# Taking the gathers of adjT's columns out of the first pass over the adjacency matrix

## The chip, the cores and the metric

The kernel runs on one core of one Trainium2 chip. The metric is the device time in microseconds (us), the median over several executions; lower is better. The engines are named as in the profile: PE is TensorE (PEld its weight loads), DVE is VectorE, ACT is ScalarE, POOL is GpSimd, SP is SyncE. "PEclk" or "clock" is the TensorE clock that was granted, as a share of full speed.

## The reference

The network has two layers over a graph of 3327 nodes with 512 features. `adj` is a dense 3327 x 3327 float32 matrix whose entries are almost all zero. What matters of it:

```python
h = jnp.maximum(_layernorm(x), 0.0)                    # layer 0: a plain GCN, dense adj used twice
h0 = jax.nn.relu(adj @ (h @ W1) + b1)                  # first pass over adj
x = x + adj @ (h0 @ W2) + b2                           # second pass over adj

h = jnp.maximum(_layernorm(x), 0.0)                    # layer 1: attention over the non-zeros of adj
hs = h @ W_sa
scores = (hs @ a_l)[:, None] + (hs @ a_r)[None, :]
e = jnp.where(adj != 0, jnp.exp(-leaky_relu(scores, 0.01)), 0.0)
attn = e / (e.sum(1, keepdims=True) + 1e-5)
x_a = attn @ hs
x_b = adj @ (h @ W_gcnb) + b_gcnb
...                                                    # two gates from adj @ h and h; cut
x = x + jax.nn.sigmoid(attn_a * x_a + attn_b * x_b)
```

## The kernel before

It works in three stages.

*Pass 1* streams the transposed matrix in column chunks of 512 (7 chunks of 26 tiles) and multiplies it. From the tiles DVE also takes, per row and group of 64 columns, the largest absolute value. Out of that, while the next chunk streams, the kernel makes *lists*: for each of 52 groups of 64 columns, which rows have any non-zero there. The lists of chunk c cover 8 groups; each group has 3 to 16 slots of 128 rows, 231 slots in all.

*Pass 2* streams the matrix again and makes `h` for layer 1, which is stored to HBM row by row (`h_dram`).

*Layer 1* is sparse. For each slot GpSimd gathers 128 rows of `h` (2080 bytes each) by an indirect DMA, and PE multiplies them with the values of adjT in that group. Those values, 64 columns of 128 listed rows (256 bytes each), have been gathered ahead of time into `adj_c`: one indirect DMA per slot, 231 as well. They are called *column gathers* below, and those of `h` *row gathers*.

In the kernel before, a column gather is written down as soon as its list is:

```python
def make_lists(c, most):
    ...                                               # flags, counts, offsets; cut
    for batch in batches:                             # groups of this chunk
        ...
        nc.vector.tensor_copy(row_h[:, f0 : f0 + m], jb[:, :m])
        nc.vector.scalar_tensor_tensor(               # row_a: rows of adjT seen as (j, group) rows
            row_a[:, f0 : f0 + m], jb[:, :m], float(NG), group_col[:, f0 : f0 + m],
            op0=ALU.mult, op1=ALU.add,
        )
        for b in batch:
            for k in range(room[b]):
                r = first[b] + k
                gather(adj_c[b][:, k, :], adj_groups, row_a[:, r : r + 1], NP * NG - 1)
        yield
```

Both passes take a step of the lists after a tile. Pass 2 also makes a block of `h` of the chunk before after every fifth tile, with four scores on DVE:

```python
for c in range(NCH):                                  # pass 1
    for j in range(NB):
        a = load_adj(j, c, "a1")
        nc.tensor.matmul(acc[:, :w], u[j], a[:, :w], ...)
        nc.vector.tensor_reduce(most[:, : w // GW, j], ..., op=ALU.max, apply_absolute_value=True)
        ...
        if j >= 2:
            next(lists, None)                         # lists of chunk c - 1
    ...

for c in range(NCH):                                  # pass 2
    for j in range(NB):
        a = load_adj(j, c, "a2")
        nc.tensor.matmul(acc[:, :w], g[j], a[:, :w], ...)
        if c == 0 and j >= 2:
            next(lists, None)                         # lists of the last chunk
        ...

def make_h1(c, sT):                                   # per block of 128 rows, in pass 2
    ...
    nc.sync.dma_start(h_dram[i * P : (i + 1) * P, :], h)
    for s, k in ((0, 0), (2, 1), (3, 2)):
        score(i, h[:, :D], s, node[i][:, k : k + 1])  # DVE, two 128x512 operands
```

In layer 1 the gathered rows go through a ring of 10 buffers, and the blocks of 128 nodes are taken in an order of their own:

```python
for c in range(n):
    hr = h_rows[taken % NH]                           # NH = 10
    taken += 1
    r = first[b] + c0 + c
    gather(hr, h_dram[:, :], row_h[:, r : r + 1], NP - 1)
    ...

blocks = [*range(1, NB // 2), 0, *range(NB // 2, NB)]
```

## Time and profile before

| | before |
|---|---|
| time, median of 3 runs | 941.31 us (936.98 to 942.03) |
| the profiled run, its span | 1143.1 us, 1141.4 us |
| busy in that span | PE 76%, DVE 56%, POOL 46%, ACT 17% |
| mean granted clock in it | 0.882 |
| column gathers (231) in that trace | start at 103.5, end at 473.3 us |
| `h` stored completely | 649 us, when the first row gather starts |
| indirect DMA, start to start | 1.30 us |

The span in 40 equal slices of 28.5 us, busy share of each in tenths:

```profile
PE   5788406356364754999999369899999789999995
...
POOL 6842766575564645400000166556555555544410
...
DMA  7688216345362543999998665556445543545421
```

Pass 1 fills slices 1 to 15. Its PE digits fall to 0 and 3 although PE is what it works with, and the DMA is low in the same slices, while POOL, which from the fifth slice on does nothing there but gather columns, keeps its 4 to 7. Slices 16 to 22 are pass 2; from the 17th, in which the last column gathers end, PE stands at 9 and the DMA at 8 or 9. The zeros of POOL there are its wait for `h`. The rest is layer 1. The profiled run is 202 us longer than the median of the timed ones.

### The profile page before, as it was taken

What the parts mean: (1) busy time and instruction counts of PE and PEld (TensorE: products, weight loads), DVE (VectorE), ACT (ScalarE), POOL (GpSimd) and SP (SyncE); (2) the same over time, 40 slices, a digit from 0 to 9 for tenths busy, and PEclk for the clock granted to TensorE, in tenths of its full rate; (3) what the DMA queues carried; (4) which work ended last, traced back from release to release, by engine and by line L of the source; (5) the groups of instructions that cost most, each with busy time, mean ns of one, the idle gap of its engine ahead of it and who ended that gap; (6) DMA issues with size and microseconds to landing.
All of it is one profiled execution on the core that took longest, in us unless ns stands there. A gap on an engine that the chain in (4) does not pass through costs nothing.

```text
span 1141.4 us, 10611 instructions
## 1 busy us (share of the span) xinstructions
PE 870.3 (76%) x2750; PEld 427.7 (37%) x2750; DVE 640.3 (56%) x1732; ACT 195.6 (17%) x449; POOL 528.3 (46%) x583
## 2 busy tenths in 40 slices
PE   5788406356364754999999369899999789999995
PEld 4564102122121331434344224445544345455552
DVE  6467205236161652366665645777777466777775
ACT  4460000000000000111111112222222122222221
POOL 6842766575564645400000166556555555544410
PEclk9999757577595876999999679999999889999998
DMA  7688216345362543999998665556445543545421
GB/s 240 219 281 287 73 38 213 85 137 163 89 200 80 171 138 103 301 339 362 340 358 297 197 182 145 152 152 182 138 133 156 141 138 100 147 128 149 131 69 40
DMA packets 107445, 199.62 MB, mean 175 GB/s; under 512 B 19516, under 2 KB 26894, under 8 KB 107376
## 3 DMA queue, kind: packets, MB, share of 16 engines
q1 hardware_dynamic: 74880, 129.64, 34.5%
q0 software_dynamic: 25872, 58.20, 18.6%
q10 hardware_dynamic: 6624, 11.02, 2.8%
q8 instruction: 24, 0.39, 0.1%
q14 instruction: 45, 0.37, 0.1%
HBM read 182.32 MB, written 27.37 MB: 184 GB/s over the span
## 4 chain that ended last, share of the span: by engine, by line
PE 52%; another core or an unknown queue 17%; DMA 11%; DVE 10%; issue 5%; POOL 3%; ACT 1%; SPq 0%; POOLq 0%; DVEq 0%; ACTq 0%
PE acc L555 13%; PE acc_g L456 11%; PE p_a L586 8%; PE p_b L586 7%; PE acc_u L371 6%; DMA a<-in_adjT_dram 5%; DVE most L372 4%; PE px L429 2%; POOL h_rows L249 2%; DMA h_rows<-h_rows,row_h 2%; PE p_s L578 2%; PE ptt L566 2%; DMA xb<-x 1%; DMA x<-in_x_dram 1%
## 5 line engine op out<-in xcount | busy, mean ns | idle before, releaser
L249 POOL DMA_INDIRECT h_rows<-h_rows,row_h x231 | 239.7, 1038 | 375.5 <-DMA h_rows<-hrow 176.1
L249 POOL DMA_INDIRECT adj_c<-in_adjT_dram,row_a x231 | 230.9, 999 | 159.5 <-issue 76.1
L555 PE MATMUL acc<-h_rows,ae 128*128 128x512 f32 x462 | 216.6, 612 | 26.5 <-DVE ae L520 19.4
L371 PE MATMUL acc_u<-a,u 128*128 128x512 f32 (+1 forms) x364 | 193.0, 663 | 5.3 <-ACT u L184 3.4
L456 PE MATMUL acc_g<-a,g 128*128 128x512 f32 (+1 forms) x364 | 158.4, 582 | 8.0 <-DMA a<-in_adjT_dram 6.0
L555 PEld LDWEIGHTS acc<-h_rows,ae 128*128 128x128 f32 x462 | 87.8, 196 | 129.8 <-issue 117.5
L372 DVE TENSOR_REDUCE most<-a 128x8 f32<-128x512 f32 (+1 forms) x182 | 112.7, 639 | 18.4 <-DMA a<-in_adjT_dram 14.8
L514 DVE TENSOR_SCALAR ae<-s_left,h_rows 128x64 f32<-128x64 f32 x231 | 55.9, 262 | 87.4 <-DMA h_rows<-h_rows,row_h 78.8
L456 PEld LDWEIGHTS acc_g<-a,g 128*128 128x128 f32 x364 | 66.7, 193 | 90.1 <-issue 48.6
L586 PE MATMUL p_a<-W_sa_sb,tyT 128*128 128x512 f32 x208 | 99.6, 622 | 0.0
L586 PE MATMUL p_b<-W_g_sb,tyT 128*128 128x512 f32 x208 | 93.5, 592 | 0.0
L321 PE MATMUL p_list<-step,at 128*128 128x27 bf16 x231 | 17.4, 184 | 94.6 <-DVE at L316 44.9
L371 PEld LDWEIGHTS acc_u<-a,u 128*128 128x128 f32 x364 | 70.2, 219 | 51.1 <-issue 40.8
L508 DVE RECIPROCAL va<-vb 128x512 f32<-128x512 f32 x26 | 87.2, 3353 | 0.9
L417 DVE SCALAR_TENSOR_TENSOR junk<-hrow,w_rows 128x512 f32<-128x512 f32 x104 | 71.8, 690 | 3.5 <-DMA x<-x 0.3
L321 PEld LDWEIGHTS <-at 128*128 128x128 bf16 x231 | 15.2, 105 | 140.9 <-issue 59.8
L193 PE MATMUL pg<-ident,gT 128*128 128x128 f32 x26 | 6.2, 376 | 75.1 <-ACT gT L190 54.8
L190 ACT ACTIVATE gT<-acc_u,b_col 128x512 f32<-128x512 f32 (+1 forms) x7 | 4.6, 657 | 332.4 <-remote 241.6
L586 PEld LDWEIGHTS p_b<-W_g_sb,tyT 128*128 128x128 f32 x208 | 39.5, 190 | 49.9 <-issue 49.9
L431 DVE TENSOR_TENSOR x<-px,xb 128x512 f32<-128x512 f32 x26 | 17.8, 683 | 70.4 <-PE px L429 70.4
L519 ACT ACTIVATE ae<-ae 128x256 f32<-128x256 f32 (+1 forms) x70 | 26.2, 379 | 170.9 <-DVE ae L518 93.4
L586 PEld LDWEIGHTS p_a<-W_sa_sb,tyT 128*128 128x128 f32 x208 | 38.8, 197 | 38.5 <-issue 38.5
(108 smaller groups left out, 894.3 us busy)
## 6 DMA issues: line engine op xcount, KB each, us to landing
a<-in_adjT_dram SPq DMA_DIRECT2D x312, 256.0 KB
h_rows<-hrow SPq DMA_DIRECT2D x26, 260.0 KB
x<-in_x_dram SPq DMA_DIRECT2D x26, 256.0 KB
xb<-x SPq DMA_DIRECT2D x26, 256.0 KB
xb<-xb SPq DMA_DIRECT2D x26, 256.0 KB
a<-in_adjT_dram SPq DMA_DIRECT2D x52, 128.0 KB
x<-x ACTq DMA_DIRECT2D x26, 256.0 KB
x1b<-x SPq DMA_DIRECT2D x26, 256.0 KB
```

The costliest lines, as they stand in the source:

```text
L249: nc.gpsimd.indirect_dma_start(out=dst, out_offset=None, in_=table, in_offset=bass.IndirectOffsetOnAxis(ap=rows, axis=0), bounds_check=las ...
L321: nc.tensor.matmul(plv[:, first[b] - f0 + s0 + k, :], at[:, k * P : (k + 1) * P], step[:, b - g0, :], start=True, stop=True,)
L371: nc.tensor.matmul(acc[:, :w], u[j], a[:, :w], start=(j == 0), stop=(j == NB - 1))
L372: nc.vector.tensor_reduce(most[:, : w // GW, j], a[:, :w].rearrange("p (b i) -> p b i", i=GW), axis=AX.X, op=ALU.max, apply_absolute_value ...
L417: nc.vector.scalar_tensor_tensor(junk, h, 1.0, w_rows[:, s, :], op0=ALU.mult, op1=ALU.mult, accum_out=into)
L429: nc.tensor.matmul(px, sT[:, b * P : (b + 1) * P], W2_sb, start=True, stop=True)
L456: nc.tensor.matmul(acc[:, :w], g[j], a[:, :w], start=(j == 0), stop=(j == NB - 1))
L508: nc.vector.reciprocal(va, vb)
L514: nc.vector.tensor_scalar(e, s_l, s_r, LEAST_SCORE, op0=ALU.add, op1=ALU.max)
L519: nc.scalar.activation(e, e, AF.Exp, scale=-1.0)
L555: nc.tensor.matmul(acc, ae[:, c, :], hr[:, :D], start=(c0 + c == 0), stop=(c0 + c == room[b] - 1),)
L586: nc.tensor.matmul(p, tyT[:, k, s, :], w_sb[:, k, :], start=(k == 0), stop=(k == KD - 1))
```

## The change

The intent: the column gathers share the DMA engines with pass 1's loads, in whose stretch the profile shows the holes. So none of them is to lie in pass 1. The column gathers become a generator, in the order in which layer 1 will want them. Of the 231, the first, of the last group (whose list is made at the start of pass 2), is a marker; 140 are drawn behind it, and the other 90 one after every second row gather of layer 1.

```diff
+EARLY = 140
...
+    def gather_adj():
+        for b in groups[-1:] + groups[:-1]:
+            for k in range(room[b]):
+                r = first[b] + k
+                yield gather(adj_c[b][:, k, :], adj_groups, row_a[:, r : r + 1], NP * NG - 1)
+
+    columns = gather_adj()
...                                                   # in make_lists:
-                for b in batch:
-                    for k in range(room[b]):
-                        r = first[b] + k
-                        gather(adj_c[b][:, k, :], adj_groups, row_a[:, r : r + 1], NP * NG - 1)
...                                                   # in pass 2, c == 0, after the last lists:
+                with tc.issue_after(next(columns).ins):
+                    for _ in range(EARLY):
+                        next(columns)
...                                                   # in combine:
                     gather(hr, h_dram[:, :], row_h[:, r : r + 1], NP - 1)
+                    if taken % 2 == 0:
+                        next(columns, None)
```

`issue_after` binds only the 140 to the marker. Nothing binds the other 90, and the scheduler is free to move those forward as far as their inputs allow.

More of the change, by code (lines that the diff above doesn't have):

```diff
@@ L116, in ln_relu, with gather @@
         nc.scalar.activation(dst, src, AF.Relu, bias=ln[:, 4:5], scale=ln[:, 3:4])
+    def gather(dst, table, rows, last):
+        return nc.gpsimd.indirect_dma_start(
+            out=dst, out_offset=None, in_=table,
+            in_offset=bass.IndirectOffsetOnAxis(ap=rows, axis=0),
+            bounds_check=last, oob_is_err=False,
+        )
+    adj_groups = adjT.rearrange("j (b i) -> (j b) i", i=GW)
+    blocks = [*range(1, NB // 2), 0, *range(NB // 2, NB)]
+    groups = [2 * i + k for i in blocks for k in range(2)]
+    def gather_adj():
[4 more added lines that the diff above has]
+    columns = gather_adj()
     with (
@@ L246, in make_constants @@
                 nc.gpsimd.memset(t, 0.0)
-        def gather(dst, table, rows, last):
-            nc.gpsimd.indirect_dma_start(
-                out=dst, out_offset=None, in_=table,
-                in_offset=bass.IndirectOffsetOnAxis(ap=rows, axis=0),
-                bounds_check=last, oob_is_err=False,
-            )
-        adj_groups = adjT.rearrange("j (b i) -> (j b) i", i=GW)
         def make_lists(c, most):
@@ L596 @@
         turning, weighing = None, None
-        blocks = [*range(1, NB // 2), 0, *range(NB // 2, NB)]
-        for n, b in enumerate(2 * i + k for i in blocks for k in range(2)):
+        for n, b in enumerate(groups):
             if b % 2 == 0:
```

## The prediction

> **What bounds the kernel now.** I read the times before the page. The three plain runs have a median of 941.3 us; the profiled run took 1143.1 us with a span of 1141.4 us. Profiling itself therefore added about 202 us, and the first thing to find out is where. The chain that ended last, by engine:
>
> ```profile
> span 1141.4 us, 10611 instructions
> ...
> PE 52%; another core or an unknown queue 17%; DMA 11%; DVE 10%; issue 5%; POOL 3%; ACT 1%; SPq 0%; POOLq 0%; DVEq 0%; ACTq 0%
> ```
>
> On one core there is no other core. The same chain in order of time puts every long piece of that 17% (194 us) between 117 and 452 us; the longest (start, length):
>
> ```profile
> 136.28 34.94 another core or an unknown queue
> ...
> 280.87 27.51 another core or an unknown queue
> ...
> 335.50 27.14 another core or an unknown queue
> ...
> 392.23 18.01 another core or an unknown queue
> ```
>
> Stretches of the core, one stalled, one clean, both in pass 1, and one in pass 2 (columns as the first line names them):
>
> ```profile
> core 0: us, PE busy (x) PEld busy (x) DVE busy (x) ACT busy (x) POOL busy (x), PEclk, DMA share, GB/s
> 135.00:172.00 37.00, 4.90 (x8) 1.91 (x8) 2.08 (x6) 0.69 (x1) 23.92 (x24) 0.55 0.16 40
> ...
> 310.00:335.00 25.00, 23.73 (x81) 9.92 (x79) 21.87 (x51) 0.00 (x0) 12.53 (x13) 0.93 0.75 230
> ...
> 505.00:535.00 30.00, 28.92 (x69) 12.03 (x68) 19.27 (x59) 5.36 (x11) 0.00 (x0) 1.00 1.00 358
> ```
>
> In the stall nothing but the gathers moves. PE's last matmul is recorded as ending at 140.0, yet its semaphore steps on at 140.4, 145.3, 150.9 and 171.2, and all others wait for those steps. These stalls look like gathers hurting pass 1, and are surely what the change is aimed at. But 1141 - 194 = 947, and a plain run, less the 1.7 us by which the profiled time exceeds its span, is 939.6. So I choose to read the stalls as made by profiling, not as time of the plain kernel.
>
> The plain timeline, then, worked out from the trace. Layer 1 runs from its first gather of rows at 649.4 to 1141.4, 492 us, so in a plain run h is complete at 939.6 - 492 = 448. Pass 1 ends at 426.1 in the trace; of the 194 us, 176 lie before that, so plain at about 249. Without stalls PE (23.7 of 25 us) and DVE (21.9) bound pass 1, with the DMA at 0.75. Pass 2 is bound by DMA (share 1.00 at 358 GB/s). Layer 1 begins bound by GpSimd's gathers and soon by PE.
>
> The gathers:
>
> ```profile
> L249 POOL DMA_INDIRECT h_rows<-h_rows,row_h x231 | 239.7, 1038 | 375.5 <-DMA h_rows<-hrow 176.1
> L249 POOL DMA_INDIRECT adj_c<-in_adjT_dram,row_a x231 | 230.9, 999 | 159.5 <-issue 76.1
> ...
> 111.51 1.00 POOL L249 DMA_INDIRECT adj_c<-in_adjT_dram,row_a  x1 [0.30 <-issue]
> 112.82 0.99 POOL L249 DMA_INDIRECT adj_c<-in_adjT_dram,row_a  x1 [0.32 <-issue]
> ...
> 649.38 1.00 POOL L249 DMA_INDIRECT h_rows<-h_rows,row_h  x1 [176.12 <-DMA h_rows<-hrow]
> ```
>
> Successive starts lie 1.30 us apart, so 231 cost GpSimd 231 x 1.303 = 301 us. In the trace they end at 473.3, and GpSimd then waits 176 us for h. That slack is partly the profile's: in a plain run the gathers go from 103.5 without a break (the lists of later column chunks come faster than GpSimd works them off) to about 405, leaving 448 - 405 = 43 us. Also, only (249 - 103.5) / 1.303 = 112 of the 231 lie under pass 1 even before the change.
>
> **What the Trainium skill says.** "Perfetto Trace Analysis", section "GPSIMD Engine Instruction", calls GpSimd's spans unreliable and advises start-to-start spacing; I use 1.303 us instead of the row's 999 ns. Its section "Tensor Engine Instruction (MATMUL, LD_WEIGHTS)" says that a matmul's end is estimated; the trace agrees, with semaphore steps up to 31 us after the recorded end. "DMA: Bandwidth & Descriptors", section "Issuing engines are not separate DMA queues", says that DMAs of all issuers share the same 16 engines; so a gather in a full pass 2 takes time from the loads. In the stall 23 gathers took 8.1% of 16 engines' time over 35 us, 0.123 us of all engines each.
>
> **The change part by part.** Of PE, DVE, ScalarE and SyncE the built program keeps every instruction in its place; GpSimd has the same instructions, and only the 231 gathers of adj are reordered. What matters is where the scheduler put them, and it is not what the change says: all 231 still stand before the first gather of rows. Only the 140 bound to the marker gather of the last group are held back. The 90 free ones had inputs early and were hoisted to the front. The new order: 7 of group 1, then 74 of groups 26 to 47, then the marker's group and the others held back (141 in all), then 9. So 81 stay in pass 1's part of the queue, none goes between layer 1's gathers.
>
> 1. GpSimd loses time. The 7 can start at 108.9 (group 1's list) and end at 118. The next need the list of chunk 3, made while chunk 4 streams. From the last matmul of chunk 0 (91) to 249 there are 5.5 chunks, 28.7 us each; chunk 3 is loaded at 91 + 3 x 28.7 = 177, and the list of group 26 takes some 7 of 26 steps more: 185. GpSimd idles from 118 to 185, 67 us, while in the kernel before it was gathering groups 0 to 25.
> 2. From 185 the other 224 follow without a break: 74 take 96 us, more than the lists of chunks 3 to 5 need; the marker's list is then done. The end is 185 + 224 x 1.303 = 477.
> 3. The first gather of rows stands behind them in the same queue, so it starts at 477 instead of 448: +29 us on the path.
> 4. Given back: before, the first gather of rows took 7.2 us until DVE used it (649.4 to 656.6), beside the weights' loads and the last scores, against 3.4 us for a later one (666.4 to 669.8). With those out of the way some 4 us return.
> 5. DMA: before, 231 - 112 = 119 gathers lay beyond pass 1; after, 231 - 7 - (249 - 185) / 1.303 = 175 do. The 56 more cost pass 2 56 x 0.123 = 7 us, which delays h to 455. This lies beside GpSimd's later end, so it is not added. Pass 1 isn't DMA-bound and gains at most a few us.
>
> Layer 1 can't make up a late start: its early blocks wait for gathers at 1.30 us each, and then PE runs gapless, so a shift passes to the end. Sum: 941.3 + 29 - 4 = 966. I take 3 us off for a gather's spacing that may be a little shorter in a plain run: **963 us**.
>
> **The rivals.**
> - The stalls are real in plain runs, and taking gathers out of pass 1 removes them. For: they occur only while gathers run. Against: 947 fits 939.6 without them; for a plain run to hold them, the rest would have to run 200 us faster, though pass 2 is already at 358 GB/s and PE at full granted clock. Were 40 us of them left, the two gather-free chunks might save 15 us: about 925 without the late start of layer 1.
> - The gathers are hidden anyway. If the plain spacing were 1.17 us, the end would be 185 + 262 = 447, and only the 7 us of DMA in pass 2 would show: 945 to 948. For: the profile slows other things, so perhaps GpSimd. Against: spacing is 1.30 both inside stalls and in clean stretches, for both kinds of gather.
> - Gathers slow down beside a full DMA. Each waits for the landing of the eighth before it. Against: the last ones, at 465 to 473 in pass 2, kept 1.30. Were they 1.4, the end would be 499 and the time about 985.
>
> **Range and chances.** The time is 941 plus the larger of two delays: DMA (about 5) and GpSimd's end (224 x spacing + 185 - 448, less 4). A spacing of 1.2 to 1.33 gives 943 to 970; uncertainty in the 448 and 185 adds some 8 either way. Range 940 to 977. The border of 2% is 960.1, near my estimate: slower 0.56, same 0.39, faster 0.05.
>
> **What would show it.** In the profile after: about 81 gathers ahead of pass 2 or at its edge, with a long idle stretch of GpSimd after the first 7; no gather of adj between gathers of rows; the wait of the first gather of rows for h (176 us before) gone or short, since the queue is late instead; chunks 1 and 2 of pass 1 free of the unknown waits, which reappear where the gathers now are. The profiled span may even shrink while the plain time grows. I am wrong if the plain time falls below 930 (stalls were real), or if GpSimd still waits long for h in a plain-length timeline (gathers cheaper than 1.30 us).

## The result, and the profile after

The changed kernel takes **975.08 us** (973.69 to 975.74, 4 runs) against 940.65 us (936.98 to 942.03, 4 runs). A ratio in this document is the mean time of one kernel's fast runs over that of the other's of the same rounds, so it is not quite the ratio of the medians: here 1.037, with a 95% interval of 1.0338 to 1.0403. The change makes the kernel slower. Its profiled run took 975.2 us, no longer than the timed ones.

The span, and the chain that ended last, by engine and by line, from the page of the changed kernel:

```profile
span 973.5 us, 10580 instructions
...
PE 49%; issue 16%; POOL 15%; DMA 12%; DVE 6%; ACT 1%; SPq 0%; POOLq 0%; DVEq 0%; ACTq 0%
PE acc L570 15%; POOL adj_c L120 11%; PE acc_u L381 10%; PE p_a L601 8%; PE p_b L601 8%; DMA a<-in_adjT_dram 5%; DMA h_rows<-h_rows,row_h 4%; PE p_s L593 2%; POOL h_rows L120 2%; PE ptt L581 2%; DMA x<-in_x_dram 1%; DMA xb<-x 1%; DVE most L382 1%; DVE va L521 1%; POOL x L187 1%
```

The 17% of "another core or an unknown queue" is gone. In its place stand POOL's column gathers (11%) and "issue" (16%), which alternate: followed piece by piece, the chain goes from one column gather to the next all the way from 249 to 485 us. The 40 slices, now of 24.3 us:

```profile
PE   4778999998999999880047899999978999999994
...
POOL 6951200377777777777767545646455564454400
...
DMA  7688898997999999984156544555464444544410
```

PE and DMA have no holes in pass 1 (slices 1 to 10), and pass 2 (slices 10 to 18) is full too. Then PE has two slices, the 19th and 20th, with hardly any work (digits 0 and 0), while POOL goes on at 7. That is the new piece. The stretches, with columns as in the prediction's table of stretches:

```profile
91.00:120.00 29.00, 26.86 (x127) 11.95 (x126) 27.29 (x74) 0.69 (x1) 7.25 (x7) 1.00 0.89 288
265.10:297.80 32.70, 31.11 (x73) 12.63 (x72) 19.95 (x61) 5.67 (x11) 25.39 (x25) 1.00 1.00 347
320.00:400.00 80.00, 73.88 (x173) 30.10 (x172) 49.86 (x157) 15.19 (x30) 62.03 (x60) 1.00 1.03 353
446.00:485.00 39.00, 0.00 (x0) 0.00 (x0) 0.00 (x0) 1.48 (x2) 29.86 (x31) 0.50 0.27 70
790.00:890.00 100.00, 100.00 (x328) 51.22 (x326) 77.57 (x182) 26.25 (x62) 47.48 (x46) 1.00 0.47 136
```

The first is chunk 1 of pass 1, with 7 column gathers, the second chunk 1 of pass 2, the third the middle of pass 2: DMA share 1.03 and 353 GB/s with 60 gathers in 80 us, so pass 2 was full as before. From 446 to 485 PE and DVE do nothing at all and GpSimd gathers 31 times. `h` was complete by then (the last store was issued at 443.2). Later PE is busy for all of 100 us, so a late start of layer 1 isn't made up there. GpSimd in the order of time, where its first long idle ends:

```profile
117.17 0.99 POOL L120 DMA_INDIRECT adj_c<-in_adjT_dram,row_a  x1 [0.30 <-issue]
183.07 1.00 POOL L120 DMA_INDIRECT adj_c<-in_adjT_dram,row_a  x1 [64.91 <-DVE at L330]
184.38 1.00 POOL L120 DMA_INDIRECT adj_c<-in_adjT_dram,row_a  x1 [0.31 <-issue]
```

After the seventh gather GpSimd waits 65 us for the list of the next group in its queue. And where the columns end and the rows begin:

```profile
483.68 1.00 POOL L120 DMA_INDIRECT adj_c<-in_adjT_dram,row_a  x1 [0.30 <-issue]
484.98 1.00 POOL L120 DMA_INDIRECT h_rows<-h_rows,row_h  x1 [0.30 <-issue]
486.29 1.00 POOL L120 DMA_INDIRECT h_rows<-h_rows,row_h  x1 [0.30 <-issue]
```

The first row gather waits 0.30 us, as any gather does behind another. In the profile of before it waited 176 us for `h`. The groups of gathers, as the page has them (busy time, mean ns of one, idle before and what ended most of it):

```profile
L120 POOL DMA_INDIRECT h_rows<-h_rows,row_h x231 | 238.8, 1034 | 197.5 <-PE acc L570 114.7
L120 POOL DMA_INDIRECT adj_c<-in_adjT_dram,row_a x231 | 240.9, 1043 | 160.9 <-issue 68.0
```

The column gathers' mean is 1043 ns, against 999 ns in the profile of before.

### The profile page after: what moved, and what is told of

It is laid out like the page before. It is cut to its first block, busy times and chain, and to the rows that moved or that the text cites. A ratio compares the mean times of both kernels' runs of the same rounds, so it can differ in the third digit from the quotient of the medians.

```text
span 973.5 us, 10580 instructions
## 1 busy us (share of the span) xinstructions
PE 831.2 (85%) x2750; PEld 412.6 (42%) x2750; DVE 637.1 (65%) x1732; ACT 195.7 (20%) x449; POOL 537.4 (55%) x583
## 4 chain that ended last, share of the span: by engine, by line
PE 49%; issue 16%; POOL 15%; DMA 12%; DVE 6%; ACT 1%; SPq 0%; POOLq 0%; DVEq 0%; ACTq 0%
PE acc L570 15%; POOL adj_c L120 11%; PE acc_u L381 10%; PE p_a L601 8%; PE p_b L601 8%; DMA a<-in_adjT_dram 5%; DMA h_rows<-h_rows,row_h 4%; PE p_s L593 2%; POOL h_rows L120 2%; PE ptt L581 2%; DMA x<-in_x_dram 1%; DMA xb<-x 1%; DVE most L382 1%; DVE va L521 1%; POOL x L187 1%
## 5 line engine op out<-in xcount | busy, mean ns | idle before, releaser
L120 POOL DMA_INDIRECT h_rows<-h_rows,row_h x231 | 238.8, 1034 | 197.5 <-PE acc L570 114.7
L120 POOL DMA_INDIRECT adj_c<-in_adjT_dram,row_a x231 | 240.9, 1043 | 160.9 <-issue 68.0
L381 PE MATMUL acc_u<-a,u 128*128 128x512 f32 (+1 forms) x364 | 164.3, 581 | 8.0 <-ACT u L207 4.8
L466 PE MATMUL acc_g<-a,g 128*128 128x512 f32 (+1 forms) x364 | 156.7, 573 | 10.3 <-DMA a<-in_adjT_dram 9.4
L601 PE MATMUL p_a<-W_sa_sb,tyT 128*128 128x512 f32 x208 | 96.8, 607 | 0.0
L381 PEld LDWEIGHTS acc_u<-a,u 128*128 128x128 f32 x364 | 60.8, 190 | 49.2 <-issue 31.7
L187 POOL TENSOR_TENSOR x<-x,b_row 128x512 f32<-128x512 f32 x26 | 33.0, 1280 | 24.5 <-ACT h L117 13.0
L575 ACT COPY ty<-acc 128x512 f32<-128x512 f32 x52 | 30.2, 582 | 61.7 <-PE acc L570 61.5
L204 PE MATMUL pu<-W_sb,hT 128*128 128x128 f32 x208 | 30.7, 294 | 9.3 <-ACT hT L198 9.2
L581 PEld LDWEIGHTS ptt<-ident,ty 128*128 128x128 f32 x208 | 26.3, 142 | 27.8 <-issue 25.1
```

Of the source, the lines that this page charges most:

```text
L120: return nc.gpsimd.indirect_dma_start(out=dst, out_offset=None, in_=table, in_offset=bass.IndirectOffsetOnAxis(ap=rows, axis=0), bounds_ch ...
L187: nc.gpsimd.tensor_tensor(xs[i], xs[i], b2_row, ALU.add)
L204: nc.tensor.matmul(pu[:, :HID], hT[:, k, :], W1_sb[:, k, :], start=(k == 0), stop=(k == KD - 1))
L381: nc.tensor.matmul(acc[:, :w], u[j], a[:, :w], start=(j == 0), stop=(j == NB - 1))
L466: nc.tensor.matmul(acc[:, :w], g[j], a[:, :w], start=(j == 0), stop=(j == NB - 1))
L581: nc.tensor.transpose(pt[:, k * P : (k + 1) * P], ty[:, k * P : (k + 1) * P], ident)
```

## The experiments

My theory after the result: the kernel lost its time because the late queue of gathers delays the first row gather, as predicted, and the size was off because gathers ran at 1.35 us instead of 1.30. Rivals: the cost is in the moved code or order rather than in the late queue; the gathers slow down because the DMA is full; and the holes in the profile of before are real and would be worth something.

The runs went to four chips: 15, 4, 2 and 5. **The kernel before took 1131 to 1142 us in all timed runs on chip 15, 928 to 941 on chip 4, 1141 to 1148 on chip 2 and 1130 to 1144 on chip 5.** All of those are labelled "fast", since that label compares a run with the fastest of the same kernel in the same call. I call a chip *stalling* where the kernel before takes some 1140 us, and *free of stalls* where it takes some 935; kernels are compared only within a call. The record of the prediction (937 to 942) is of the second kind.

### On stalling chips: first call (chip 15)

**Before again**, unchanged, one look:

> The kernel before, unchanged, profiled once more. If the 194 us of waits on an unknown queue were an accident of the first profiled execution or of profiling, this profile may show a span near 939 us: then I expect the last column gather to end at about 405 to 412 us, h to be complete (first gather of rows) at 447 us (give or take 4), and a wait of 35 to 43 us of GpSimd before it. If the stalls belong to this order of gathers whenever it is profiled, the span is again above 1100 us with most waits in pass 1. If they were real in plain runs, the plain time could not be 941.

1128.53 us for the run whose profile was kept. The seven timed runs of the same kernel beside it took 1131.12 to 1142.47 us. So the kept profile is no longer than the runs that are timed on the same chip, and my reading of the first profile's holes is not borne out: by their length the timed runs of this chip have them too. (Each of these runs lists a span and a granted clock. So the record does not say of any of them that nothing was recorded while it ran, and whether recording has a part in the stalls stays open.) Pass 1 ends at 415.3 us in this trace and `h` is complete at 637.7, much as in the profile of before (426.1 and 649.4). That profile therefore looks like one of a stalling chip, while the times beside it are of a chip free of stalls.

**No hold**, the changed kernel with the 231 gathers drawn at once, so that each goes as soon as its list is there:

```diff
-                with tc.issue_after(next(columns).ins):
-                    for _ in range(EARLY):
-                        next(columns)
+                for _ in columns:
+                    pass
```

> The changed kernel, with nothing held behind the marker gather: all 231 column gathers are free at the same place of the code, and the scheduler puts them in the order in which lists are ready, without an idle stretch, nearly as in the kernel before. If the late start of layer 1 (GpSimd idle for 66 us, then 224 gathers in a row) is the whole loss, this is 940 us (936 to 945, ratio 0.995 to 1.005). If another part of the change costs the time (code moved, gathers beside pass 2), it stays near 975.

1125.29 us, ratio to before 0.9901 (0.9844 to 0.9958). The gathers run from 103.7 to 461.9 without a long idle (13.2 us at most), pass 1 ends at 416.7, `h` is complete at 636.1: as before. It is 1% faster than the kernel before on this chip, by more than its interval; on chip 2 (below) it is not.

**Hold 125** and **hold 110** hold back fewer, and draw the rest right after them:

```diff
-EARLY = 140
+EARLY = 125      # and 110
...
                     for _ in range(EARLY):
                         next(columns)
+                for _ in columns:
+                    pass
```

> 125 held instead of 140: 15 more column gathers (of groups 0 and 1) run at once when their list is ready, in GpSimd's idle stretch. 209 instead of 224 are left at 183 us, so at 1.348 us each the queue ends at 465 instead of 485 and the time is 955 (952 to 959): 20 us less than the changed kernel, 1.35 us per gather. If the loss comes from DMA traffic in pass 2, 15 gathers fewer there give 1 to 2 us: 973.

> 110 held: 29 instead of 7 gathers run before 183 us, 202 are left, the queue ends at about 455 and the time is 945 (941 to 949); it can't get below 940 since h is complete only at about 446. If the loss comes from DMA traffic in pass 2, about 972.

1153.91 us, 1.0142 (1.0068 to 1.0216), and 1148.55 us, 1.0113 (1.005 to 1.0176). Their absolute numbers miss by some 200 us, because the expectations were written for a chip free of stalls. Nor can the dose be read from the ratios: on this chip the gathers end at 501.2 and 495.7 us, but `h` is complete only at 662.3 and 654.5, so the queue's lateness costs nothing, and what differs is when `h` is complete, 17 to 25 us later than in the kernel before (637.7). The series was made to measure the late queue, and didn't.

### On a chip free of stalls: second call (chip 4)

The kernel before took 935.6 us there (928.21 to 940.9, 7 runs).

**Small groups first.** The kernel before with layer 1's blocks in another order. Those with few slots (and so less GpSimd time per unit of PE work) go first:

```diff
-        blocks = [*range(1, NB // 2), 0, *range(NB // 2, NB)]
+        blocks = [*range(NB // 2, NB), *range(1, 7), 0, *range(7, NB // 2)]
```

> The kernel before with layer 1's blocks in another order: those of 3 and 4 columns first, then blocks 1 to 6, 0, 7 to 12. It tests the claim that layer 1 starts bound by GpSimd's gathers at 1.3 us each and that PE is gapless afterwards: with few gathers per block PE gets its matmuls by the weights at once. If so some 20 us of the start are saved: 920 us (910 to 932). If the start's idle PE is latency that any order has, 938 to 945.

934.61 us (931.41 to 939.01), ratio 0.9989 (0.9926 to 1.0053): no gain, a miss. PE was indeed busier at the start of layer 1, 57.96 us of the first 71.6 against 47.47 of the first 72 in the changed kernel. It lost that again later, and layer 1 took 488.9 us against 488.5. So my step "then PE runs gapless" was too simple: layer 1's length did not react to a better beginning.

The run is worth more as a view of the kernel before free of stalls, since nothing ahead of layer 1 differs from it. GpSimd at the end of the columns:

```profile
412.94 0.99 POOL L249 DMA_INDIRECT adj_c<-in_adjT_dram,row_a  x1 [0.30 <-issue]
448.39 0.99 POOL L249 DMA_INDIRECT h_rows<-h_rows,row_h  x1 [34.45 <-DMA h_rows<-hrow]
```

The columns end at 413.9 us, GpSimd waits 34.45 us for `h`, and the first row gather starts at 448.4. That is the timeline that the prediction worked out from the stalled trace (end at about 405, 43 us of slack, `h` at 448). Set beside the changed kernel's 485.0, it gives the shift: 36.6 us, against a measured 34.4 us (975.08 - 940.65). The other stages leave no room for a second loss: pass 1 ends at 241.7 us here and at 239.6 in the changed kernel, the last store of `h` is issued at 445.5 and 443.2, and layer 1 takes 488.9 and 488.5. What differs is the time between the last store and the first row gather, 2.9 us here and 41.8 there. That answers the rival of the moved code, although "no hold" was never run on a chip free of stalls.

**No column gathers** at all in the kernel before (wrong; the relative error is 0.046):

```diff
-                for b in batch:
-                    for k in range(room[b]):
-                        r = first[b] + k
-                        gather(adj_c[b][:, k, :], adj_groups, row_a[:, r : r + 1], NP * NG - 1)
```

> Wrong result on purpose: the kernel before without any column gather (the compact columns stay zero). It bounds what any placement of the gathers can win. If they lie wholly beside other work and cost only DMA share under pass 2 (chunks of pass 2 took 30 us beside gathers in the changed kernel's profile, 28.4 without in the profile of before), 934 us (929 to 940). If gathers in pass 1 really stall it, as the profile of before suggests, well below 920.

930.56 us (924.47 to 935.64), ratio 0.9942 (0.9865 to 1.002). All 231 together cost the kernel before about 0.6% (the interval includes nothing at all), and by the interval's lower end no more than 1.4%, so on such a chip no placement of them can win more than that. It also prices them in the DMA: pass 2, from its start to the last store of `h`, takes 199.3 us without any, 203.3 with 126 of them (small groups first) and 202.9 with 180 (the changed kernel), in one trace each.

**The intent enforced.** In the built kernel none of the 90 went between the row gathers. Here each is bound to its row gather:

```diff
-                    gather(hr, h_dram[:, :], row_h[:, r : r + 1], NP - 1)
+                    got = gather(hr, h_dram[:, :], row_h[:, r : r + 1], NP - 1)
                     if taken % 2 == 0:
-                        next(columns, None)
+                        with tc.issue_after(got.ins):
+                            next(columns, None)
```

> What the change says, enforced: 141 column gathers after the last list, the other 90 each queued behind a gather of rows (one after every two), none in pass 1. The 141 end at about 250 + 141 x 1.36 = 442 us, just before h is complete, so layer 1 starts on time at 446. But then GpSimd needs (180 + 90) x 1.305 = 352 us for the first 180 gathers of rows, to 798, and some 165 us of work follow the 180th: 965 us (957 to 975). If the intent of the change is sound and only the scheduler spoiled it, 940 or less.

998.7 us (995.76 to 999.31), ratio 1.0676 (1.0616 to 1.0736): slower than the changed kernel, and slower than I expected by over 20 us. Layer 1 started on time, at 446.0. From there two row gathers and a column gather took 3.905 us, three times 1.302. But the 270 gathers of that mixture took until 835.9, 390 us, where 270 x 1.302 is 352. The groups of gathers of this kernel:

```profile
L120 POOL DMA_INDIRECT adj_c<-in_adjT_dram,row_a x231 | 240.3, 1040 | 235.7 <-DVE row_a L351 165.5
L120 POOL DMA_INDIRECT h_rows<-h_rows,row_h x231 | 238.2, 1031 | 147.8 <-PE acc L571 80.4
```

and stretches of its layer 1:

```profile
446.00:550.00 104.00, 70.57 (x167) 32.87 (x168) 42.71 (x133) 16.88 (x46) 78.59 (x78) 0.79 0.52 145
750.00:850.00 100.00, 86.94 (x235) 42.48 (x234) 57.40 (x144) 20.01 (x48) 65.60 (x64) 0.90 0.42 116
```

GpSimd still waits 80.4 us for PE to give row buffers back. Yet PE is busy for only 86.94 us of the 100 from 750 to 850, where it had 100 of 100 in the changed kernel from 790 to 890. My reading is that with a ring of 10 rows GpSimd can't use its idle time to run ahead: it waits where PE is the slower of the two, and PE waits where GpSimd is, and the column gathers lengthen the second without filling the first. No run has a deeper ring, so this is read from the waits and not shown. In the changed kernel the row gathers show 114.7 us of waiting for PE, and it was tempting to read that as room for 90 x 1.3 = 117 us of other gathers.

**No scores.** In the changed kernel three of the four scores per block are left out and their results set to zero, so that DVE has less to do in pass 2 (the output still passed the tolerance, though it is not the reference's computation):

```diff
+    for t in node:
+        nc.gpsimd.memset(t, 0.0)
...
-                for s, k in ((0, 0), (2, 1), (3, 2)):
-                    score(i, h[:, :D], s, node[i][:, k : k + 1])
```

> Wrong result on purpose: the changed kernel without three of the four scores of a row (they stay zero), so DVE has three two-operand instructions fewer per block of pass 2. In the changed kernel's profile 77 of 462 gathers took over 1.08 us, nearly all beside these scores, and spacing under pass 2 was 1.365 instead of 1.303 us. If DVE's two-operand work slows GpSimd's gathers, spacing falls to about 1.32, the queue ends some 8 us earlier and the time is 967 (964 to 970). If the full DMA slows them, spacing stays at 1.36 and the time at 973 to 976.

964.25 us (963.69 to 972.64, 5 runs), ratio 1.0314 (1.0258 to 1.037). The expected 964 to 970 held, and the rival's 973 to 976 didn't come. The gain against the changed kernel is less sure than that sounds: the medians differ by 10.8 us, but the ratios to the kernel before (1.037 and 1.0314) differ by only 0.6%, some 5 us; the interval of the second reaches to 1.037, so by the times alone a gain isn't shown. The trace says 5 too: the mean spacing of the 224 gathers after the idle stretch went from 1.348 to 1.324 us, 5.4 us in all, and of the 231 column gathers those of over 1.08 us went from 53 to 15. One run, the profiled one, took 972.64, 8 us more than the other four; I don't know why. Four column gathers of the changed kernel, and what DVE did beside them (each with start, length, and idle before):

```profile
428.60 1.22 POOL L120 DMA_INDIRECT adj_c<-in_adjT_dram,row_a  x1 [0.30 <-issue]
430.13 1.16 POOL L120 DMA_INDIRECT adj_c<-in_adjT_dram,row_a  x1 [0.31 <-issue]
431.59 1.24 POOL L120 DMA_INDIRECT adj_c<-in_adjT_dram,row_a  x1 [0.30 <-issue]
...
434.60 1.00 POOL L120 DMA_INDIRECT adj_c<-in_adjT_dram,row_a  x1 [0.30 <-issue]
```

```profile
428.99 0.69 DVE L427 SCALAR_TENSOR_TENSOR junk<-hrow,w_rows 128x512 f32<-128x512 f32 x1
...
429.72 0.69 DVE L427 SCALAR_TENSOR_TENSOR junk<-hrow,w_rows 128x512 f32<-128x512 f32 x1
```

and of the kernel without the scores, a gather beside the one score that it still has, and one in the same stretch as above:

```profile
277.78 0.69 DVE L430 SCALAR_TENSOR_TENSOR junk<-hrow,w_rows 128x512 f32<-128x512 f32 x1
277.83 1.51 POOL L123 DMA_INDIRECT adj_c<-in_adjT_dram,row_a  x1 [0.30 <-issue]
...
429.05 1.00 POOL L123 DMA_INDIRECT adj_c<-in_adjT_dram,row_a  x1 [0.30 <-issue]
```

A gather beside back-to-back scores on DVE (each 0.69 us, two 128x512 operands in SBUF) took 1.16 to 1.24 us; one without them 1.00. The kept traces give the rule: where a score had begun before the gather and was still running 0.13 us after the gather's start, the gather took 1.00 us and in addition what was left of the score at that moment. In the lines above the score of 429.72 ends at 430.41, 0.15 us after 430.13 + 0.13, and the gather of 430.13 took 1.16; the one of 277.78 ends at 278.47, 0.51 us after 277.83 + 0.13, and the gather took 1.51. The 0.13 is fitted; with it the sum holds within 5 ns for all 51 such gathers of the changed kernel, and for 39 of 39 with small groups first. (In the kernel without the scores three gathers whose score began only 0.015 us before them were not held up.) Of the 11 gathers beside which DVE's addition with one operand in PSUM (`x<-px,xb`) was running at that moment none was slow. The expectation's "nearly all beside these scores" was too much, though: of the 77 slow gathers 24 are row gathers of layer 1, after the last score.

The Trainium skill states in "SBUF — State Buffer", section "SBUF: two separate sides", that DVE and GpSimd share a pair of SBUF ports, which a DVE operation with two SBUF inputs holds against a GpSimd operation that reads SBUF, and that the loser then blocks fully until the end. The trace agrees, in the size too: the gather, which takes its row numbers from SBUF, is late by the whole rest of the score, 0.16 to 0.24 us in the lines of the changed kernel and 0.51 us in the last pair.

### The dose again, on chips that turned out to stall: third and fourth call (chips 2 and 5)

The series again, with the same edits as above: **no hold** and **hold 110** on chip 2, then **hold 110** and the **changed kernel** itself on chip 5.

> The free order again, since the first call ran on a chip on which the kernel before itself took 1138 us instead of 936 to 942, so that its ratios can't be set beside the changed kernel's 975. On a chip where before takes 935 to 942: ratio to before 1.00 (0.993 to 1.007) if the late start of layer 1 is the whole loss; 1.037 if it is something else in the change.

> 110 held instead of 140, again. On a chip where before takes 935 to 942: the queue of column gathers ends at about 455 us instead of 485, ratio 1.006 (1.000 to 1.010), that is some 30 us below the changed kernel. If DMA traffic under pass 2 is the loss, 1.033. On a chip where before takes 1138 us this can't be told.

> 110 held instead of 140, a third time, now beside the changed kernel on the same chip. On a chip where before takes 935 to 942: queue of column gathers done at about 455 us, ratio to before 1.006 (1.000 to 1.012). If DMA traffic under pass 2 is the loss, 1.033. On a chip where before takes about 1140: 1.009 to 1.011 as in the two runs so far.

> The changed kernel again. On a chip where before takes 935 to 942: ratio 1.037, some 30 us over hold_110. On a chip where before takes about 1140: there the gathers cost the same stall wherever they stand (in hold_125 and hold_110 it moved from pass 1 into pass 2 undiminished), so if the stall belongs to each gather the ratio is 1.01 to 1.03 and the profile shows a wait of more than 140 us within pass 2 and none after the first 7 gathers in pass 1; if the stall comes from gathers beside pass 1 alone, well below 1, near 1000 us.

Both chips stalled. Measured: no hold 1143.99 us, 0.9987 (0.9932 to 1.0042); hold 110 1155.86 us, 1.0091 (1.0053 to 1.0128) on chip 2 and 1147.4 us, 1.0074 (0.9997 to 1.0152) on chip 5; the changed kernel 1150.42 us (1147.49 to 1154.6), 1.0107 (1.0026 to 1.0189). Moving the code alone costs nothing there (0.9987). The changed kernel's ratio lies where it was expected if the stall belongs to each gather (1.01 to 1.03). On chips free of stalls the dose stays unmeasured.

The changed kernel on a stalling chip is the test of the change's own intent. Three stretches of it, the second chunk of pass 1 and the first two of pass 2:

```profile
121.00:150.60 29.60, 27.64 (x100) 11.64 (x99) 24.92 (x71) 0.69 (x1) 0.00 (x0) 0.94 0.88 286
282.20:326.10 43.90, 29.08 (x77) 12.46 (x78) 5.89 (x26) 0.00 (x0) 29.95 (x30) 0.81 0.61 182
326.10:506.70 180.60, 52.88 (x74) 16.36 (x73) 18.25 (x57) 5.74 (x11) 139.16 (x137) 0.56 0.32 83
```

Pass 1 is clean where no gather runs: 29.6 us for a chunk, 27.64 of PE. The chunk from 326.1 on, in pass 2, takes 180.6 us, with the DMA at 0.32 and 83 GB/s and 137 gathers; the same chunk took 32.7 us on the chip of the record, with the DMA at 1.00. The gathers themselves are no slower here (1.33 us from start to start, against 1.37 in that chunk). Nor is a load slow once it is issued; the lines of SP and PE in the stalled chunk:

```profile
400.81 0.33 SPq L154 DMA_DIRECT2D a<-in_adjT_dram  x1
...
403.87 2.07 PE L466 MATMUL acc_g<-a,g 128*128 128x512 f32 x2 [3.90 <-DMA a<-in_adjT_dram]
406.42 5.92 SPq L154 DMA_DIRECT2D a<-in_adjT_dram  x2
...
409.30 2.08 PE L466 MATMUL acc_g<-a,g 128*128 128x512 f32 x2 [3.36 <-DMA a<-in_adjT_dram]
```

PE starts on a tile 3.0 us after its load was issued (median), against 6.1 us in the unstalled pass 2. It is the issue that is late. The tiles go through a ring of 8 buffers (`adjp`, `bufs=8`), and in pass 2 only PE reads them, so SP can issue a load as soon as PE is done with the tile of eight loads before. In the unstalled pass 2 it does so 0.9 us (median) after the recorded end of that tile's matmul, in this chunk 39 us after it; before these loads SP waits for a step of PE's semaphore for 126 of the 181 us. So what PE has finished reaches SP late, and PE then waits for each single load. This is the lateness that the prediction saw in the first profile, where a step of PE's semaphore came 31 us after the last matmul. The traces of stalling runs have a second mark: where gathers run, records of semaphore steps are missing (801 for 925 steps of PE in the first profile; the changed kernel's trace of the record has them all). Whether the two have one cause no run tells.

Against the unstalled chip, pass 1 here is 41 us longer (280.7 against 239.6) and pass 2 up to the last store 175 us (377.4 against 202.9). In the kernel before, again on a stalling chip, it is pass 1 that is 174 us longer (415.3 against 241.7 in the kernel with small groups first) and pass 2 only 16. So the stall goes with the column gathers wherever they stand, and moving them moves it. The row gathers do not bring it: layer 1 takes 487 to 493 us on both kinds of chip (the enforced kernel aside), though few loads run beside them.

No version that I ran, with a right result, beats the kernel before by more than its interval, except "no hold" on chip 15 (1%, and not on chip 2).

## Why the prediction was right or wrong

**Where the gathers go: right.** The built order gave it: 7 gathers, an idle stretch, and all 231 ahead of the first row gather. The idle stretch was put at 118 to 185 us and lay at 118 to 183.1. Layer 1 ran with no column gather in it.

**The late queue sets the start of layer 1: right.** The wait of the first row gather for `h` went from 34.45 us (the kernel before without stalls) to 0.30. The columns end 70.8 us later (484.7 instead of 413.9), the slack of 34.45 us takes its part of it, and so the first row gather moved from 448.4 to 485.0. Nearly all of that, 34.4 of 36.6 us, arrived at the end. The reason given for that, PE without a gap, is only half right. PE had gaps in the changed kernel's layer 1 too (89.78 us busy from 690 to 790), and layer 1 kept its length even with a better start.

**The spacing: mis-sized.** The term 224 x 1.303 = 292 us measured 224 x 1.348 = 302 us, so the end came at 485 instead of 477, although the start was 2 us early. The scores of DVE make nearly all of the difference: of the 10.3 us by which the changed kernel's spacings exceed 1.303, 9.9 stand at its 53 slow gathers, and 50 of these are scores' (without three of the four scores the spacing is 1.324, and most of the 15 slow gathers left stand beside the fourth). I had read the 1.303 in a stalled trace, in which hardly any column gather meets a score: 3 of 231 are slow there. Free of stalls the order of before has 1.344 as well (small groups first), so the slower pace is not the change's. The 3 us that I took off for a shorter spacing had the wrong sign. The given-back 4 us came out as 36.6 - 34.4 = 2.2. The 8 us of later end, the 3 and about 2 are roughly the 12 between 963 and 975. (Two of the prediction's side sums are off by 2 to 3 us: by its own formula a spacing of 1.33 gives 972 and not 970, and one of 1.4 gives 988 and not 985. The estimate of 963 does not rest on them.)

**The DMA: mis-sized.** I priced a gather in pass 2 at 0.123 us of all engines, 7 us for 56 of them. The trace shows nothing of it: the last store of `h` is issued at 443.2 us with 180 gathers in pass 2, at 445.5 with 126. Only against none at all is pass 2 some 4 us longer. Since I had not added the term, the time was not affected.

**"I choose to read the stalls as made by profiling": not borne out.** The arithmetic, 1141 - 194 = 947 next to a plain 939.6, was sound, but it compared a profile with times of another kind of chip. Timed runs of the same kernel take 1130 to 1148 us on three of the four chips of the experiments. What the choice did was to remove the stalls, which the chip of the timed runs did not have, and so the number survived for a reason that was not the one given: that is luck. The chain's label, "an unknown queue", would have fitted either reading, and I had no run that could tell them apart. Nor do the 31 us from a matmul's recorded end to the step of its semaphore show that the end is an estimate, as I put it: in the changed kernel's trace every step of PE comes within 0.015 us of a recorded end. The 31 us are the stall itself.

**The rivals.** "The stalls are real, and the change removes them" is half true: they are real, on some chips, and the change doesn't remove them even there (1.0107 on chip 5). "Hidden anyway" fell with the 39 us of idle PE. "Gathers slow down beside a full DMA" was right about slower gathers and wrong about the cause: where they are slow it is the scores beside them, and at 320 to 400 us with the DMA at 1.03 39 of 59 were not slow.

**What stays open.** Why a chip stalls and another doesn't; each was met in one call, so it could also be a state of the hour and not of the chip. Why PE's steps reach the others late there while column gathers run, and whether the recording of the runs has a part in it. And how the time on a chip free of stalls goes with the number of gathers held back: neither "no hold" nor a part of the 140 was run on one.

## What to carry to other kernels

Read a queue as a queue: work that is moved behind a late input holds up everything after it on that engine, and here 65 us of idle GpSimd turned into 35 us at the end, once its slack of 34 us was used up. Look at the built order, not at the source, to see where a scheduler puts unbound instructions; and don't count an engine's total idle time as room for other work, since with a shallow ring it may be idle only where it could not have run ahead. Take an instruction's pace from a stretch in which the engines beside it work as they will in the end: the 1.303 us came from a stalled trace. When a profiled run and the timed runs differ by 20%, run the kernel again, timed and profiled on the same chip, before you explain either of them.

## What the Trainium skill lacked or had wrong

- No page has it: chips, or states of a chip, that differ by a fifth in this kernel's time at an unchanged program. Before took 928 to 941 us on one chip and 1130 to 1148 on three others. In pass 2 of the changed kernel on one of the latter, beside column gathers, a load was issued 39 us after PE had left its buffer instead of 0.9, and 83 GB/s moved over 180 us, against 347 GB/s in the same chunk elsewhere. Layer 1 with its row gathers took no longer there.
- "Perfetto Trace Analysis" has no remark on a wait whose release the trace doesn't hold (the viewer calls it "another core or an unknown queue"). On a single core such waits made 17% of the span of before, and the timed runs on such chips were as long as the profiled one.
- "SBUF — State Buffer" doesn't say when in an indirect DMA GpSimd needs the shared ports: here 0.13 us after its start, a fit that holds within 5 ns in 51 of 51 gathers, and a gather then took 1.00 us and the rest of DVE's two-operand instruction, up to 1.51 us in all.
- "DMA: Bandwidth & Descriptors", section "Issuing engines are not separate DMA queues": that all issuers share the engines is right, but it doesn't price it. 180 gathers in a pass 2 with the DMA at 1.0 left it at 202.9 us, against 199.3 with none, so by one trace each about 0.02 us a gather (0.03 with 126 gathers).
- No page that I found gives the pace of gathers: 1.30 us from start to start for 128 rows, whether a row has 256 or 2080 bytes, where no score is beside them.
